# Fourteen mixed-input tiles transposed by VectorE and transfers instead of TensorE, and a last projection in two column halves

## The chip, the cores and the metric

The kernel runs on one core of a Trainium2 chip. The metric is the device time of one execution in microseconds (us), given as the median of several runs. Engines are named as in the profile: PE is TensorE's matmul, PEld its weight load, DVE is VectorE, ACT is ScalarE, POOL is GpSimd, SP is SyncE. "ACTq" and "SPq" are the sequencers of ACT and SP, on which their DMAs are issued.

## What is computed

The reference adds two terms to `x` (64 sequences of 32 tokens of 512 numbers). The first mixes the 32 tokens of a sequence by one of 16 condition matrices. The second is attention of the result over a paged cache of 512 keys plus the 32 new ones, with 32 query heads and 8 key heads of 128.

```python
x = x + einsum('bct,bcd->bdt', x, weights[condition])        # the mix: x1
q, k, v = x1 @ Wq.T, x1 @ Wk.T, x1 @ Wv.T                    # q, k: rmsnorm, then rope
k_all = concat([k_cache[block_table], k]); v_all likewise    # cache masked beyond its length
o = softmax(q @ k_all / sqrt(128)) @ v_all
x = x1 + o @ Wo.T
```

## The kernel before

All data are float32. The 64 sequences are taken four at a time, as tiles of 128 tokens: 16 tiles. Each tile is worked on twice, once for each half of the heads (`hh` is 0 or 1), so there are 32 steps; `st.n` counts them, and steps 0 to 15 are the first half. In a step the four sequences of the tile are four batches (`bt`), and each batch has four key heads (`g`), which makes 16 slots (`slot = bt * GH + g`). Every slot has the scores and the values of one batch and head. Into the slots the kernel places, by hand, the work of other steps: the projections of the step after this one (`ahead`, through `pieces`: rotation tables in slot 2, `k_a` in slot 3, the query projections `q_a` in slots 4 to 7, `v_a` in slot 13), the output projection of the step before in slots 8 and 9, and the mixed input of the step after next (`beyond`) in slots 14 and 15.

The order of instructions on PE and SP is the order in which the program writes them (`manual_schedule`); DVE, ACT and POOL are ordered by a scheduler. A DMA that SP issues is held until the data that it needs are there, and everything behind it on SP's queue waits too. The program gives DMAs of SP and ACT eight semaphores in turn; a DMA waits until the one that had its semaphore before has landed.

These parts matter here:

- `x1_a` loads a tile of `x` into `acc`. `x1_c` (slot 14) multiplies it on PE by a block-diagonal matrix `bd` of four conditions (L363) and DVE adds the product to `acc` (L364). `acc` now holds x1 with tokens on the partitions.
- `x1_b` (slot 15) makes `x1t`, x1 with its 512 columns on the partitions in four blocks of 128: four PE transposes (L371), an ACT copy out of PSUM (L373), and an ACT-issued DMA that keeps it in device memory for the second half of the heads (`x1t_d`, L374).
- `x1_t` (slot 13) loads `x1t` again for a step of the second half (L357). For a step of the first half it does nothing.
- `project` multiplies `x1t`, as the stationary operand, by a weight tile (L407). `k_a` in slot 3 of the next step is its first user.
- `load_k`, called when a `Batch` is made, has SP load 16 pages of 64 KB of cached keys (L294) into one of two buffers; page numbers come by a register load (L286). The keys are copied to DVE-written tiles by `head_keys` (L567) one batch ahead of their use. The batch made at `bt == 3` has half of its pages issued in slot 13.
- `turn_rows` (L457) and `spread` (L471) already turn the queries of steps 2 and later by DVE in 32x32 blocks, and SP transfers put the blocks in place.
- The tile tag `w1` is one buffer, used by `norm_rope`, the rotation angles and `count`.
- The last output projection runs after the loop, all 512 columns at once (L520). Three quarters through it calls `in_range`, which counts the softmax denominators that are in range, sums the counts on PE (L1020) and writes the flag `redo` (L1021). DVE then adds the projection to `acc` (L528) and SP stores it (L533). All engines read `redo` and branch on it; the slower exact version behind the branch is not run here.

Of the kernel before, what the change touches and what calls it, by code (L numbers as in the profile page):

```python
# [11 lines left out]
F32 = mybir.dt.float32  # L12
I32 = mybir.dt.int32
AF = mybir.ActivationFunctionType
ALU = mybir.AluOpType
# [4 lines left out]
P = 128  # L20
B, S, HID = 64, 32, 512
D, HQ, HK = 128, 32, 8
REP = HQ // HK
PAGES, PSIZE, NPP = 64, 32, 16
# [31 lines left out]
def cond_resid_paged_attention_kernel(  # L56
# [130 lines left out]
    def steps_of(exact, pools):  # L187
# [164 lines left out]

        def x1_t(st):

            if st.hh:
                st.x1t = work.tile([P, KC, P], F32, tag="x1t", name=f"x1t_{st.name}", bufs=1)
                nc.sync.dma_start(st.x1t.rearrange("p c q -> p (c q)"), x1t_d[st.t])  # L357

        def x1_c(st):
            if st.hh:  # L360
# [5 lines left out]
        def x1_b(st):  # L366
            if st.hh:
                return
            pm = ps_p.tile([P, KC, P], F32, tag="pp", name=f"px1t_{st.name}")
            for c in range(KC):  # L370
                nc.tensor.transpose(pm[:, c, :], st.acc[:, c * P : (c + 1) * P], ident)  # L371
            st.x1t = work.tile([P, KC, P], F32, tag="x1t", name=f"x1t_{st.name}", bufs=1)
            nc.scalar.copy(st.x1t, pm)  # L373
            nc.scalar.dma_start(x1t_d[st.t], st.x1t.rearrange("p c q -> p (c q)"))  # L374

        def rot_tables(st):

# [98 lines left out]
        def by_tensor(st):  # L476
            return st.n < 2 or exact
# [32 lines left out]
        def q_b(st, g):  # L510
            to_columns(st, g)

        def out_proj(st, part, halfway=None):

            if part.start == 0:
                st.po = ps_p.tile([P, HID], F32, tag="pp", name=f"pout_{st.name}")
            for i in range(part.start, part.stop):
                if halfway and i == 3 * QH // 4:
                    halfway()
                nc.tensor.matmul(  # L520
                    st.po,
                    st.ot[:, i, :],
                    wt["o", st.hh, i // 4][:, i % 4, :],
                    start=(i == 0),
                    stop=(i == QH - 1),
                )
            if part.stop == QH:
                nc.vector.tensor_tensor(st.acc, st.po, st.acc, ALU.add)  # L528
                if exact or st is steps[-1]:
                    store(st)  # L530

        def store(st):
            nc.sync.dma_start(  # L533
                out[st.t * P : (st.t + 1) * P, :] if st.hh else acc_d[st.t], st.acc
            )

        def new_ot(st):
            st.ot = act.tile([P, QH, P], F32, tag="ot", name=f"ot_{st.name}", bufs=1)
# [192 lines left out]
        if exact:  # L731
            nc.gpsimd.memset(vn_bufs[0], 0.0)
            nc.gpsimd.memset(vn_bufs[1], 0.0)
            key_no = wpool.tile([P, LK], F32, tag="key_no", name="key_no")
            key_no_i = work.tile([P, LK], I32, tag="sm", name="key_no_i")
            nc.gpsimd.iota(key_no_i, pattern=[[1, LK]], base=0, channel_multiplier=0)
            nc.vector.tensor_copy(key_no, key_no_i)
            nc.vector.memset(key_no[:, L:LK], -1e9)
            for st in steps:
                if st.t == 0:  # L740
                    load_w("k", st.hh)
                    load_w("v", st.hh)
                    for g in range(GH):
                        load_w("q", st.hh, g)
                        load_w("o", st.hh, g)
                if not st.hh:
                    load_cond_weights(st.t)
                x1_a(st)
                x1_t(st)
                x1_c(st)  # L750
                x1_b(st)
                rot_tables(st)
                k_a(st)
                k_b(st)
                v_a(st)
                for g in range(GH):
                    q_a(st, g)
                    q_b(st, g)
                new_ot(st)
                for bt in range(BT):  # L760
                    exact_batch(Batch(st, bt), key_no)
                out_proj(st, slice(0, QH))
            return
# [163 lines left out]
        for st in steps:  # L927
            ahead = steps[st.n + 1] if st.n + 1 < len(steps) else None
            beyond = steps[st.n + 2] if st.n + 2 < len(steps) else None
            fill = pieces(ahead) if ahead else {}  # L930
            for bt in range(0 if st.n else 1, BT):
                this, after = batch, None
                n = st.n * BT + bt + 2
                if n < NHH * NT * BT:
                    after = Batch(steps[n // BT], n % BT, NPP // 2 if bt == BT - 1 else NPP)
                    unfilled += [(after, c) for c in range(VC)]
                for g in range(GH):
                    slot = bt * GH + g
                    if st.n or slot > GH:
                        scores(this, g)  # L940
                    if slot == 0:
                        new_scores(st)
                    if slot in (1, 3):
                        new_values(st, slot - 1)
                    if slot < GH and valued is not None:
                        values(*valued)
                    for piece in fill.get(slot, ()):
                        if isinstance(piece, tuple):
                            piece[0](ahead, piece[1])
                        else:  # L950
                            piece(ahead)
                    if slot in (8, 9) and st.n:
                        out_proj(steps[st.n - 1], slice((slot - 8) * QH // 2, (slot - 7) * QH // 2))
                    if slot == 9:
                        if st.n:
                            new_ot(st)
                        for ba in turned:
                            turn(ba)
                        turned = []
                        if 0 < st.n < NT // TRIG - 1:  # L960
                            tmp = work.tile(
                                [P, 3, TRIG * HD], F32, tag="w1", name=f"trig_{st.n}", bufs=1
                            )
                            with tc.issue_after(last["dve"]), tc.issue_after(last["act"]):
                                angles((st.n + 1) * TRIG, tmp)
                    if slot == 10 and st.n:
                        store(steps[st.n - 1])
                    if st.n and beyond:
                        if slot == 6 and not beyond.hh:
                            load_cond_weights(beyond.t)  # L970
                        if slot == 11:
                            x1_a(beyond)
                    if slot == 13:
                        if beyond:
                            x1_t(beyond)
                        for load in after.pages_left if after else ():
                            load()
                    if slot == 14 and beyond:
                        x1_c(beyond)
                    if slot == 15 and beyond:  # L980
                        x1_b(beyond)
                    if slot == 1 and st.n == NT:
                        count(0)
                    if st.n == 1 and slot in (4, 5):
                        load_parts(outputs, 0, slot + 2)
                    for at in second_outputs.get((st.n - NT, slot), ()):
                        load_parts(outputs, 1, at)
                    if st.n in (NT - 2, NT - 1):
                        load_parts(
                            [("k", 0), ("q", 0), ("q", 1), ("q", 2), ("q", 3), ("v", 0)],  # L990
                            1,
                            slot - 5 + (st.n - NT + 2) * BT * GH,
                        )
                    for _ in range({1: 0, GH: 2}.get(slot, 1)):
                        if unfilled and (g or unfilled[0][0] is this):
                            next_values()
                    if slot >= GH and valued is not None:
                        values(*valued)
                    valued = this, g
                    if g == 1 and bt != 1:  # L1000
                        for ba in turned:
                            turn(ba)
                        turned = []
                    if later is not None:
                        head_keys(later, g)
                turned.append(this)
                batch, later = later, after
# [14 lines left out]
                redo, pc, float(P * NHH * NT * BT * GH), None, ALU.not_equal  # L1022
            )

        out_proj(steps[-1], slice(0, QH), in_range)

    redo = const.tile([1, 1], I32, tag="redo", name="redo")
    run(False)
# [54 lines left out]
```

## Time and profile before

| | |
|---|---|
| device time, median of 3 runs | 2170.74 us (2169.95 to 2174.28) |
| the profiled execution's own time | 2166.54 us |
| span of the profiled execution | 2164.8 us |
| PE busy | 2145.4 us, 99% |
| DVE, ACT, POOL busy | 1196.6, 863.0, 805.5 us |
| DMA engines, mean | 165 GB/s; 35.1% of their time for SP's queue, 22.3% for POOL's |
| granted TensorE clock | 0.997 |

The page lists the busy time of each engine, 40 slices of the span, the DMA queues, the chain of work that ended last, and groups of instructions. A group's row gives the line, the engine, the operation, the tile it writes and those it reads, the count, the busy time in us and the mean time of one in ns. PE's matmuls overlap in the records: one can last 0.27 us in its row while the next starts 0.11 us after it. What one costs is therefore read from the starts of its neighbours. A DMA's row gives the time that its issue took, not that of its data. When the data have landed is read from the times at which its semaphore was counted up in the trace.

### The profile page before, as it was taken

What the parts mean: (1) busy time and instruction counts of PE and PEld (TensorE: products, weight loads), DVE (VectorE), ACT (ScalarE), POOL (GpSimd) and SP (SyncE); (2) the same over time, 40 slices, a digit from 0 to 9 for tenths busy, and PEclk for the clock granted to TensorE, in tenths of its full rate; (3) what the DMA queues carried; (4) which work ended last, traced back from release to release, by engine and by line L of the source; (5) the groups of instructions that cost most, each with busy time, mean ns of one, the idle gap of its engine ahead of it and who ended that gap; (6) DMA issues with size and microseconds to landing.
All of it is one profiled execution on the core that took longest, in us unless ns stands there. A gap on an engine that the chain in (4) does not pass through costs nothing.

```text
span 2164.8 us, 41582 instructions
## 1 busy us (share of the span) xinstructions
PE 2145.4 (99%) x12990; PEld 1497.4 (69%) x12990; DVE 1196.6 (55%) x2884; ACT 863.0 (40%) x1576; POOL 805.5 (37%) x1009
## 2 busy tenths in 40 slices
PE   8999999999999999999999999999999999999998
PEld 5766777667776677766777766777667777667775
DVE  5666555665455564555654565644655545556442
ACT  3444444444433343333443333433334433334441
POOL 4433333433333343333433334333334333334330
PEclk9999999999999999999999999999999999999999
DMA  8665565555655556556766855565555555555651
GB/s 250 188 165 160 157 169 160 143 159 158 173 153 153 154 156 173 156 151 190 229 181 178 207 161 162 164 177 156 155 144 168 165 167 165 147 159 162 172 158 59
DMA packets 386839, 357.47 MB, mean 165 GB/s; under 512 B 54480, under 2 KB 316640, under 8 KB 386608
## 3 DMA queue, kind: packets, MB, share of 16 engines
q1 hardware_dynamic: 341616, 212.74, 35.1%
q0 software_dynamic: 41984, 137.71, 22.3%
q10 hardware_dynamic: 3008, 4.25, 0.5%
q8 instruction: 106, 1.74, 0.3%
q14 instruction: 125, 1.02, 0.2%
HBM read 302.59 MB, written 12.58 MB: 146 GB/s over the span
## 4 chain that ended last, share of the span: by engine, by line
PE 97%; DVE 1%; DMA 1%; ACT 0%; issue 0%; POOL 0%; DVEq 0%; ACTq 0%
PE po_x L632 22%; PE ps_x L574 21%; PE pout_x L520 20%; PE pp_q_x L407 20%; PE pp_v_x L407 5%; PE pp_k_x L407 5%; PE pnv_x L616 2%; PE psn_x L592 1%; PE pmix_x L363 1%; DMA pages_at<-in_pages_v_dram 1%; PE px1t_x L371 0%; DMA cond<-in_cond_dram 0%; PE pt_x L451 0%; ACT sq_q_x L417 0%; ACT q_cols_x L491 0%
## 5 line engine op out<-in xcount | busy, mean ns | idle before, releaser
L321 POOL DMA_INDIRECT raw_x<-in_vc_dram,v_row x512 | 539.6, 1054 | 821.5 <-ACT v_x L334 757.0
L582 ACT ACTIVATE pr_x<-ps_x 128x512 f32<-128x512 f32 x512 | 305.7, 597 | 822.7 <-PE ps_x L574 819.3
L632 PEld LDWEIGHTS po_x<-v_x,pr_x 128*128 128x128 f32 x4096 | 515.7, 192 | 123.9 <-issue 112.5
L632 PE MATMUL po_x<-v_x,pr_x 128*128 128x129 f32 x4096 | 550.6, 278 | 0.0
L407 PE MATMUL pp_q_x<-wq_x,x1t_x 128*128 128x512 f32 x1024 | 462.2, 594 | 0.0
L520 PE MATMUL pout_x<-wo_x,ot_x 128*128 128x512 f32 x1024 | 450.2, 593 | 0.0
L574 PE MATMUL ps_x<-q_cols_x,kh_x 128*128 128x128 f32 x3072 | 406.0, 275 | 1.6 <-ACT q_cols_x L491 1.6
L574 PEld LDWEIGHTS ps_x<-q_cols_x,kh_x 128*128 128x128 f32 x3072 | 376.3, 192 | 18.0 <-issue 14.5
L334 ACT ACTIVATE v_x<-raw_x,valid 128x512 f32<-128x512 f32 x512 | 363.2, 716 | 13.4 <-DMA raw_x<-in_vc_dram,v_row 13.2
L520 PEld LDWEIGHTS pout_x<-wo_x,ot_x 128*128 128x128 f32 x1024 | 190.0, 191 | 214.0 <-issue 213.8
L567 DVE COPY kh_x<-k_t_x 128x512 f32<-128x512 f32 x506 | 206.8, 418 | 194.6 <-PE ps_x L574 153.5
L407 PEld LDWEIGHTS pp_q_x<-wq_x,x1t_x 128*128 128x128 f32 x1024 | 185.8, 191 | 184.8 <-issue 184.8
L650 DVE TENSOR_TENSOR nv_x<-po_x,nv_x 128x258 f32<-128x258 f32 x256 | 108.6, 424 | 309.4 <-PE po_x L632 294.0
L424 POOL TENSOR_TENSOR rs_q_x<-ms_q_x,minus_half 128x4 f32<-128x4 f32 x128 | 140.0, 1094 | 168.9 <-DVE ms_q_x L422 168.9
L417 ACT ACTIVATE sq_q_x<-pp_q_x 128x512 f32<-128x512 f32 x128 | 76.4, 597 | 266.2 <-PE pp_q_x L407 179.3
L574 PE MATMUL ps_x<-q_last_x,kh_x 128*128 128x128 f32 x1024 | 135.3, 275 | 0.0
L528 DVE TENSOR_TENSOR acc_x<-pout_x,acc_x 128x512 f32<-128x512 f32 x32 | 22.2, 692 | 199.3 <-PE pout_x L520 199.3
L574 PEld LDWEIGHTS ps_x<-q_last_x,kh_x 128*128 128x128 f32 x1024 | 124.6, 192 | 0.0
L407 PE MATMUL pp_v_x<-wv_x,x1t_x 128*128 128x512 f32 x256 | 115.2, 593 | 0.0
L407 PE MATMUL pp_k_x<-wk_x,x1t_x 128*128 128x512 f32 x256 | 115.1, 593 | 0.0
L653 DVE TENSOR_TENSOR o_x<-nv_x,rden 128x256 f32<-128x256 f32 x256 | 108.8, 425 | 6.2
L421 DVE TENSOR_REDUCE ms_q_x<-sq_q_x 128x4 f32<-128x512 f32 x128 | 86.3, 674 | 45.4 <-ACT sq_q_x L417 44.8
(107 smaller groups left out, 1464.8 us busy)
## 6 DMA issues: line engine op xcount, KB each, us to landing
k_t_x<-in_kt_dram SPq DMA_DIRECT2D x2048, 64.0 KB
q_cols_x<-rows_x SPq DMA_DIRECT2D x360, 80.0 KB
q_last_x<-rows_x SPq DMA_DIRECT2D x120, 80.0 KB
raw_x<-in_vc_dram,v_row POOLq DMA_INDIRECT x512, 4.2
wo_x<-in_wo_dram SPq DMA_DIRECT2D x32, 256.0 KB
acc_x<-in_x_dram SPq DMA_DIRECT2D x16, 256.0 KB
x1t_d<-x1t_x ACTq DMA_DIRECT2D x16, 256.0 KB
acc_d<-acc_x SPq DMA_DIRECT2D x16, 256.0 KB
```

The costliest lines, as they stand in the source:

```text
L321: nc.gpsimd.indirect_dma_start(out=raw.rearrange("p g d -> p (g d)"), out_offset=None, in_=vc, in_offset=bass.IndirectOffsetOnAxis(ap=v_ro ...
L334: nc.scalar.activation(v_bufs[b % 2][:, c, :, 0:D], raw, AF.Copy, scale=ok)
L407: nc.tensor.matmul(pp, st.x1t[:, c, :], w[:, c, :], start=(c == 0), stop=(c == KC - 1))
L421: nc.vector.tensor_reduce(ms, sq, AX.X, ALU.add)
L424: nc.gpsimd.tensor_tensor(rs, ms, minus_half, ALU.pow)
L520: nc.tensor.matmul(st.po, st.ot[:, i, :], wt["o", st.hh, i // 4][:, i % 4, :], start=(i == 0), stop=(i == QH - 1),)
L567: last["dve"] = nc.vector.tensor_copy(k, ba.k_raw[:, :, g, :]).ins
L574: nc.tensor.matmul(ps[:, c, :], ba.k[g][:, c * P : (c + 1) * P], queries(ba, g), start=True, stop=True,)
L582: last["act"] = nc.scalar.activation(pr, ps, AF.Exp, scale=SCALE).ins
L632: nc.tensor.matmul(ba.po[:, g % 2, :], ba.pr[g][:, c, :], ba.v_t[:, c, g, :], start=(c == 0), stop=(c == VC - 1),)
L650: nc.vector.tensor_tensor(t, ba.po, t, ALU.add)
L653: nc.vector.tensor_tensor(ba.o[:, both, :], t[:, :, 0:D], rd.unsqueeze(2).to_broadcast([P, 2, D]), ALU.mult,)
```

## The change

For the first-half steps from number 2 on (14 of them), `x1_b` no longer uses PE and ACT. DVE transposes `acc` in 32x32 blocks into a tile of tag `w1`, and SP writes the blocks to `x1t_d` by four DMAs, one for each group of 32 partitions. Each puts 512 pieces of 32 numbers (128 bytes) in their places, so that `x1t_d` holds the full transpose. `x1_t` then loads `x1t` from there for these steps too. It stands at the start of the next step, between page 4 and page 5 of the keys that are loaded there (`bt == 0`); before, all 16 pages were issued in one go. Steps 0 and 1 keep the PE transposes, and the loads for the second half keep their place in slot 13.

The last output projection is done as two halves of 256 columns, each with its own DVE add and its own store. `in_range` is called three quarters through the first half.

```diff
         def x1_t(st):
-            if st.hh:
-                st.x1t = work.tile([P, KC, P], F32, tag="x1t", name=f"x1t_{st.name}", bufs=1)
-                nc.sync.dma_start(st.x1t.rearrange("p c q -> p (c q)"), x1t_d[st.t])
+            st.x1t = work.tile([P, KC, P], F32, tag="x1t", name=f"x1t_{st.name}", bufs=1)
+            nc.sync.dma_start(st.x1t.rearrange("p c q -> p (c q)"), x1t_d[st.t])
...
         def x1_b(st):
             if st.hh:
                 return
+            if not by_tensor(st):
+                return x1_turn(st)
...
+        def x1_turn(st):
+            turned = work.tile([P, KC * BT, S], F32, tag="w1", name=f"x1w_{st.name}", bufs=1)
+            nc.vector.transpose(turned, st.acc.rearrange("p (j d) -> p j d", d=S))
+            kept = x1t_d[st.t].rearrange("(j d) (c b x) -> b d c j x", d=S, b=BT, x=S)
+            for b in range(BT):
+                nc.sync.dma_start(
+                    kept[b],
+                    turned[b * S : (b + 1) * S, :, :].rearrange("p (c j) x -> p c j x", c=KC),
+                )
...
-        def out_proj(st, part, halfway=None):
+        def out_proj(st, part, cols=slice(0, HID), halfway=None):
...
                 nc.tensor.matmul(
-                    st.po,
+                    st.po[:, cols],
                     st.ot[:, i, :],
-                    wt["o", st.hh, i // 4][:, i % 4, :],
+                    wt["o", st.hh, i // 4][:, i % 4, cols],
...
-                nc.vector.tensor_tensor(st.acc, st.po, st.acc, ALU.add)
+                nc.vector.tensor_tensor(st.acc[:, cols], st.po[:, cols], st.acc[:, cols], ALU.add)
                 if exact or st is steps[-1]:
-                    store(st)
+                    store(st, cols)
...
             for bt in range(0 if st.n else 1, BT):
...
+                back = bt == 0 and ahead and not ahead.hh
                 if n < NHH * NT * BT:
-                    after = Batch(steps[n // BT], n % BT, NPP // 2 if bt == BT - 1 else NPP)
+                    after = Batch(
+                        steps[n // BT],
+                        n % BT,
+                        NPP // 4 if back else NPP // 2 if bt == BT - 1 else NPP,
+                    )
+                    if back:
+                        x1_t(ahead)
+                        for load in after.pages_left:
+                            load()
...
                     if slot == 13:
-                        if beyond:
+                        if beyond and beyond.hh:
                             x1_t(beyond)
...
-        out_proj(steps[-1], slice(0, QH), in_range)
+        out_proj(steps[-1], slice(0, QH), slice(0, HID // 2), in_range)
+        out_proj(steps[-1], slice(0, QH), slice(HID // 2, HID))
```

More of the change, by code (lines that the diff above doesn't have):

```diff
@@ L511, in q_b @@
             to_columns(st, g)
-        def out_proj(st, part, halfway=None):
-            if part.start == 0:
+        def out_proj(st, part, cols=slice(0, HID), halfway=None):
+            if part.start == 0 and cols.start == 0:
                 st.po = ps_p.tile([P, HID], F32, tag="pp", name=f"pout_{st.name}")
@@ L527, in out_proj, with store @@
             if part.stop == QH:
-                nc.vector.tensor_tensor(st.acc, st.po, st.acc, ALU.add)
+                nc.vector.tensor_tensor(st.acc[:, cols], st.po[:, cols], st.acc[:, cols], ALU.add)
                 if exact or st is steps[-1]:
-                    store(st)
[L532 to L535, printed above, removed]
+                    store(st, cols)
+        def store(st, cols=slice(0, HID)):
+            dst = out[st.t * P : (st.t + 1) * P, :] if st.hh else acc_d[st.t]
+            nc.sync.dma_start(dst[:, cols], st.acc[:, cols])
         def new_ot(st):
@@ L748, in steps_of @@
                 x1_a(st)
-                x1_t(st)
+                if st.hh:
+                    x1_t(st)
                 x1_c(st)
```

## The prediction

> **What bounds the kernel now.** I read the busy times first, then the chain of what ended last, then a window over the steps, and last the timeline of the slot that is changed.
>
> ```profile
> PE 2145.4 (99%) x12990; PEld 1497.4 (69%) x12990; DVE 1196.6 (55%) x2884; ACT 863.0 (40%) x1576; POOL 805.5 (37%) x1009
> ...
> PE 97%; DVE 1%; DMA 1%; ACT 0%; issue 0%; POOL 0%; DVEq 0%; ACTq 0%
> ```
>
> A busy share alone proves little, because matmul records overlap. The window over steps 2 to 14 (columns: window, length, busy time of PE, PEld, DVE, ACT, POOL with counts, clock, DMA share, GB/s) settles it: PE has no gap in 870 us.
>
> ```profile
> 170.00:1040.00 870.00, 870.00 (x5262) 605.47 (x5261) 491.12 (x1175) 357.14 (x648) 323.82 (x402) 1.00 0.57 162
> ```
>
> So work taken off PE is gained one to one, and anything that makes PE wait is lost one to one. Timeline of slots 14 to 16 and of the next step's `k_a` (start, length, engine, line):
>
> ```profile
> 502.74 0.69 DVE L364 TENSOR_TENSOR acc_x<-pmix_x,acc_x 128x512 f32<-128x512 f32 x1 [0.44 <-DMA k_t_x<-in_kt_dram]
> 503.43 1.06 PE L574 MATMUL ps_x<-q_last_x,kh_x 128*128 128x128 f32 x8
> 504.32 0.60 PE L371 MATMUL px1t_x<-ident,acc_x 128*128 128x128 f32 x4
> 504.75 1.06 PE L632 MATMUL po_x<-v_x,pr_x 128*128 128x129 f32 x8
> ...
> 515.71 1.88 PE L407 MATMUL pp_k_x<-wk_x,x1t_x 128*128 128x512 f32 x4
> ```
>
> The four transposes hold PE from 504.32 to 504.75: 0.43 us. x1 is complete at 503.43 and `x1t` is first needed by the weight load ahead of 515.71, at 515.60. These 12.17 us are what a route through device memory may take. They are 12.1 to 12.2 us in 13 of the 14 steps.
>
> [...] only loads of 128 bytes are here, of 11 ns a packet. [...] an `x1t` load lasts 0.37 us in its row and lands 3.3 us after its start.
>
> **PE's gain.** 14 steps lose four transposes: 14 x 0.43 = 6.0 us. ACT loses 14 copies (0.58) and DMA issues (0.33); it is busy 40% and nothing of PE waits for it, so that is worth nothing.
>
> **DVE.** It gains 14 transposes of 128x512, by the nearest row 0.70 us each. DVE runs at 55%; queued behind it are the adds, head copies and output turns of slot 15. The buffer freed by the add at L650 is used again about 6 us later and the key copies a batch later, so a shift of 0.7 us costs nothing. Without that cover it would be 9.8 us. The turned tile takes the one `w1` buffer; its next user in slot 4 comes some 17 us after x1 is complete, later than the four writes that read it.
>
> ```profile
> L663 DVE STREAM_TRANSPOSE ot_x<-o_x 128x512 f32<-128x512 f32 x127 | 86.1, 697 | 1.2
> ...
> L471 SPq DMA_DIRECT2D q_cols_x<-rows_x x360: 507/588/1577, 144.1 to 2085.8; - x180
> ...
> L357 SPq DMA_DIRECT2D x1t_x<-x1t_d x16: 331/372/402, 1040.2 to 2026.8; - x16
> ...
> L286 SPq TENSOR_LOAD <-pages_sb x128: 967/1004/1742, 7.1 to 2106.5; - x128
> ...
> 501.67 4.56 SPq L294 DMA_DIRECT2D k_t_x<-in_kt_dram  x8
> ```
>
> **SP's new chain**, from the moment x1 is complete (503.43 in the step shown):
> - SP is still issuing slot 13's pages until 506.23, so +2.8; over the steps from 4 on 2.6 to 4.4, mean 3.0. This hides the DVE transpose, done by +0.8.
> - Four writes. Nearest row: the spread, also from 32 partitions, 0.59 plus a gap of 0.04; from below a plain store, 0.38 with gap. I take the spread: 2.5, so +5.5.
> - The register load of the next batch, L286. Its median is 1.0, but at this boundary mostly 1.5 to 1.7; I take 1.5, and 0.26 to the first page: +7.3.
> - Four pages at a spacing of 0.51: +9.35. Here the load of `x1t` is issued, if the writes have landed.
> - Landing: the 16 loads of the second half took 2.6 to 4.9 us, median 3.3: +12.65.
>
> PE needs it at 12.17 - 0.43 = 11.74. It is **0.9 us late**, and PE waits, with nothing to do in its order behind it: 14 x 0.9 = 12.6 us. The ends: plain-store issue, register load of 1.0 and landing in 2.65 give 3.0 + 1.5 + 1.26 + 2.06 + 2.65 = +10.5, early by 1.2, cost 0. The upper ends of register load and landing give about +14.6, late by 2.9, cost 40.
>
> The writes: the fourth starts at +4.9 and holds nothing if it has landed by +9.35. Stores of the same 256 KB in one DMA (L374) took 2.0 to 5.5 us. The 14 x 2048 pieces are 128 for each of 16 DMA engines per step; at 11 ns they take 1.4 us and are hidden.
>
> The twelve remaining pages follow the load: issued by +15.9, where before the sixteenth was issued at +16.1 (519.5), because SP stood waiting for ACT's write:
>
> ```profile
> SPq L294 <- DMA x1t_d<-x1t_x: 33.2, 16, 6.5
> ```
>
> That wait goes (33 us of SP, none of it PE's), and the new one takes its place; the keys come no later. POOL's queue is not touched.
>
> **The end.** 32 half matmuls for 16: PE turns over a 128-column weight load and matmul in 0.11 us, so half the columns take half the time, and the projection stays 13.7 us. The last DVE add shrinks from 0.69 to about 0.42 (L650, 258 columns): 0.27. The count is 5.15 us sooner (12 of 32 pieces instead of 24). At the end POOL drains for 8.57 us after its branch, to 2163.91, and SP is done at 2162.56. If that drain only starts sooner, 1.35 more is gained; if it waits for something else, nothing. 0.3 to 1.6; I take 1.0.
>
> **Sum**, against the profiled execution of 2166.5: - 6.0 - 1.0 + 12.6 = + 5.6, 2172.1. The median of the runs lies 4.2 above that execution: 2170.7 + 5.6 = **2176.3 us**. 0.2% (4.3 us) is about what a measurement can tell from no change here.
>
> **Rivals.** *Hidden.* The load is there in time and only the gain is left: 2170.7 - 7.0 = 2163.7. For it: the page loads issued at that moment landed mostly in 1.8 to 2.5 us, near their fastest, and the chain's low end is 1.2 us early. Against it: the medians say late, and instruction fetches of 16 KB held SP's issue for 1 to 2 us in half of the steps near there. It decides if the chain comes to 11.74: for instance writes of 0.43 each with the gap, register load 1.25, pages 2.06 and 3.3 for landing, with little jitter. Chance 0.33.
>
> *Slow pieces.* 128-byte writes to device memory hold the load. They decide from (9.35 - 3.85) / 128 = 43 ns a piece and engine. At 64 ns they end at 12.0, the load lands near 15.5, 3.8 late, 53 us: about 2217. At the 86 ns of a 2048-byte packet: about 2257. Against it: 11 ns for loads. [...] Chance 0.2 with every other delay above 2 us a step.
>
> *Late keys.* Priced above at nothing; DVE already waits 25 us for pages without PE noticing. It needs pages over 5 us later. It lies in the 0.2.
>
> That the change doesn't do what it says is excluded: PE's order without the transposes and SP's with the four writes, the load and the twelve pages follow from the code.
>
> **Numbers.** Forecast 0.47: late by 0.3 to 2 us a step, 2168 to 2192. Hidden 0.33: 2161.5 to 2166.5. Slow 0.2: above 2192. Faster by over 0.2%: 0.28 of hidden and 0.01 = 0.29. Within: 0.05 + 0.11 + 0.04 = 0.20. Slower: 0.35 + 0.16 = 0.51. The range runs from 2162 to 2204, which leaves out the worst half of the slow case and the edge of the hidden one. Both signs are likely; the forecast's own range is 2168 to 2192.
>
> **What would show it.** In the profile after: a wait of PE's weight load at `k_a` for the DMA into `x1t`, 14 times of about 0.9 us (none: hidden; over 2: slow pieces); SP waiting ahead of that load for the writes (long: slow pieces); no px1t beyond steps 0 and 1; about 10 us more of DVE. The forecast is wrong if PE has no gap in the steps of the first half.

## The result and the profile after

The changed kernel takes 2182.59 us in the median of 7 runs (2178.88 to 2189.57), the kernel before 2171.41 us (7 runs, the three of the table above among them): ratio 1.0057, interval 1.0047 to 1.0066. It is slower by about 12 us. Its profiled execution took 2179.96 us, with a span of 2178.2 us. Lines have moved: in the changed kernel the mix's add is L363, the DVE turn L381, the four writes L384, the load of `x1t` L356, `k_a` (and the other projections) L420, the page loads L294 as before, the last projection L533 with its add L541.

The page of the kernel after: busy times, the chain of what ended last, and the group of `k_a`'s matmuls (busy us, mean ns | idle time before them, and what ended it).

```profile
PE 2144.7 (98%) x12966; PEld 1498.1 (69%) x12966; DVE 1205.7 (55%) x2899; ACT 860.1 (39%) x1562; POOL 804.8 (37%) x1009
...
PE 91%; SPq 3%; DMA 2%; issue 1%; DVE 1%; ACT 1%; POOL 0%; DVEq 0%; ACTq 0%
...
L420 PE MATMUL pp_k_x<-wk_x,x1t_x 128*128 128x512 f32 x256 | 118.8, 607 | 11.5 <-DMA x1t_x<-x1t_d 9.0
```

PE's share of the chain fell from 97% to 91%, and SP's queue and DMAs now have 5% together, where they had 1%. The row of `k_a` had no idle time before; now it has 11.5 us, most of it put down to the load of `x1t`. (The page counts from the modelled end of the matmul before; by the starts of the matmuls, which are used below, the same waits come to 13.5 us.) The rest of the 11.5 us is put down to ACT's copies `nv` and `v`, but those had long been done when PE went on: the load was what came last there too. The window over steps 2 to 14 of the kernel after says the same, with PE busy 858.63 of 870 us:

```profile
170.00:1040.00 870.00, 858.63 (x5141) 592.66 (x5140) 494.43 (x1179) 346.51 (x625) 319.13 (x398) 1.00 0.58 162
```

The timeline of the same step as in the prediction, from the mix to `k_a`:

```profile
506.23 3.43 SPq L294 DMA_DIRECT2D k_t_x<-in_kt_dram  x7
...
506.82 0.69 DVE L363 TENSOR_TENSOR acc_x<-pmix_x,acc_x 128x512 f32<-128x512 f32 x1 [0.44 <-PE pmix_x L362]
...
507.61 0.71 DVE L381 STREAM_TRANSPOSE x1w_x<-acc_x 128x512 f32<-128x512 f32 x1
...
509.76 3.50 SPq L384 DMA_DIRECT2D x1t_d<-x1w_x  x4
...
514.65 1.90 SPq L294 DMA_DIRECT2D k_t_x<-in_kt_dram  x4
...
516.74 0.33 SPq L356 DMA_DIRECT2D x1t_x<-x1t_d  x1
...
519.64 1.52 PE L420 MATMUL pp_k_x<-wk_x,x1t_x 128*128 128x512 f32 x3
```

x1 is complete at 507.51 and turned at 508.32, but SP issues pages until 509.66, then the four writes, a register load, four pages, and only at 516.74 the load, which lands at 519.51; PE goes on at 519.64. That is 0.3 us late, and this is one of the mild steps: over the 14 the wait is between nothing and 2.8 us. And SP's waits (us in total, times, longest):

```profile
SPq L294 <- DMA x1t_d<-x1t_x: 5.5, 1, 5.5
...
SPq L356 <- DMA x1t_d<-x1w_x: 2.4, 4, 1.0
```

The old wait for ACT's write has gone from 33.2 to 5.5 us. The new one, ahead of the load, is 2.4 us in all, in 4 waits: in at least ten of the 14 steps the writes had landed.

When the starts of PE's groups are laid beside those of the kernel before, one profiled execution against the other, the 13.4 us between them fall into these parts:

| part | us | forecast |
|---|---|---|
| transposes gone, 14 x 0.44 | - 6.1 | - 6.0 |
| PE waiting at the 14 `k_a` | + 13.5 | + 12.6 |
| slower matmuls just after those waits | + 2.7 | none |
| last projection and end | - 1.2 | - 1.0 |
| first 105 us (startup) | + 1.5 | none |
| second half of the heads, up to the last projection | + 3.0 | none |

The last two rows are not of the change: the experiments below show them in kernels that don't have it, or with another size in each execution. The 1.5 us of the start arise between 60.37 and 63.79 us, where the granted clock is 0.50 in this trace and 1.00 in the profile of before.

In the third row 1.8 us come from one place. After a wait of 2.84 us PE ran its next four matmuls at 0.85 us apiece instead of 0.43. Two windows there (the third figure from the end of a row is the granted clock):

```profile
995.50:999.00 3.50, 3.48 (x5) 1.42 (x6) 0.00 (x0) 0.00 (x0) 0.00 (x0) 0.52 0.72 216
999.50:1003.00 3.50, 3.50 (x16) 2.07 (x15) 1.45 (x4) 1.73 (x4) 0.08 (x1) 1.00 0.29 82
```

The clock was 0.52 for 3.5 us, though PE was busy in them, and 1.00 again afterwards. The mean over the execution, 0.997 as before, doesn't show it. The other 0.9 us are 0.07 us between the first two matmuls of each of the other 13 `k_a`.

The end of the kernel after:

```profile
2161.09 1.99 PE L533 MATMUL pout_x<-wo_x,ot_x 128*128 128x256 f32 x8
...
2163.12 0.42 DVE L541 TENSOR_TENSOR acc_x<-pout_x,acc_x 128x256 f32<-128x256 f32 x1 [1.78 <-PE pout_x L533]
...
2163.60 7.17 PE L533 MATMUL pout_x<-wo_x,ot_x 128*128 128x256 f32 x32 [0.52 <-DVE acc_x L541]
2170.81 0.42 DVE L541 TENSOR_TENSOR acc_x<-pout_x,acc_x 128x256 f32<-128x256 f32 x1 [7.27 <-PE pout_x L533]
```

Both halves lie in one PSUM tile, so the second half of the matmuls stood still until DVE had read the first: the last of the first half ends its turn at 2162.92, the next starts at 2163.60. From its first to its last matmul the projection took 1.1 us longer, 0.7 us of it by this wait. Against that, the stretch from the last matmul's start to the end of the span is 7.8 us instead of 10.1. POOL's drain again took 8.57 us, but it began 5.8 us before the last matmul, where it had begun 0.7 us after it, and so it no longer ends last: the last store landed 3.6 us after the last matmul's start, and SP's closing waits took another 4.2 us.

### The profile page after: what moved, and what is told of

Read it like the earlier page. It is cut to its first block, busy times and chain, and to the rows that moved or that the text cites. A ratio compares the mean times of both kernels' runs of the same rounds, so it can differ in the third digit from the quotient of the medians.

```text
span 2178.2 us, 41737 instructions
## 1 busy us (share of the span) xinstructions
PE 2144.7 (98%) x12966; PEld 1498.1 (69%) x12966; DVE 1205.7 (55%) x2899; ACT 860.1 (39%) x1562; POOL 804.8 (37%) x1009
## 4 chain that ended last, share of the span: by engine, by line
PE 91%; SPq 3%; DMA 2%; issue 1%; DVE 1%; ACT 1%; POOL 0%; DVEq 0%; ACTq 0%
PE pout_x L533 20%; PE pp_q_x L420 20%; PE po_x L644 19%; PE ps_x L586 19%; PE pp_k_x L420 5%; PE pp_v_x L420 4%; PE pnv_x L628 2%; SPq L294 2%; PE psn_x L604 1%; DMA x1t_x<-x1t_d 1%; SPq L384 1%; SPq L484 1%; DMA pages_at<-in_pages_v_dram 1%; DMA x1t_d<-x1w_x 0%; SPq L286 0%
## 5 line engine op out<-in xcount | busy, mean ns | idle before, releaser
L420 PE MATMUL pp_q_x<-wq_x,x1t_x 128*128 128x512 f32 x1024 | 461.3, 593 | 0.0
L533 PE MATMUL pout_x<-wo_x,ot_x 128*128 128x512 f32 (+1 forms) x1056 | 450.5, 580 | 0.5 <-DVE acc_x L541 0.5
L533 PEld LDWEIGHTS pout_x<-wo_x,ot_x 128*128 128x128 f32 x1056 | 195.7, 190 | 210.0 <-issue 207.6
L420 PEld LDWEIGHTS pp_q_x<-wq_x,x1t_x 128*128 128x128 f32 x1024 | 185.2, 191 | 184.5 <-issue 184.0
L541 DVE TENSOR_TENSOR acc_x<-pout_x,acc_x 128x512 f32<-128x512 f32 (+1 forms) x33 | 22.3, 676 | 204.8 <-PE pout_x L533 204.8
L420 PE MATMUL pp_k_x<-wk_x,x1t_x 128*128 128x512 f32 x256 | 118.8, 607 | 11.5 <-DMA x1t_x<-x1t_d 9.0
L420 PE MATMUL pp_v_x<-wv_x,x1t_x 128*128 128x512 f32 x256 | 115.2, 592 | 0.0
L434 DVE TENSOR_REDUCE ms_k_x<-sq_k_x 128x4 f32<-128x512 f32 x32 | 22.0, 686 | 163.2 <-ACT sq_k_x L430 163.2
```

Source lines behind the costliest of these rows:

```text
L420: nc.tensor.matmul(pp, st.x1t[:, c, :], w[:, c, :], start=(c == 0), stop=(c == KC - 1))
L434: nc.vector.tensor_reduce(ms, sq, AX.X, ALU.add)
L533: nc.tensor.matmul(st.po[:, cols], st.ot[:, i, :], wt["o", st.hh, i // 4][:, i % 4, cols], start=(i == 0), stop=(i == QH - 1),)
```

## The experiments

The theory after the comparison: the new route costs what SP's queue makes it cost. The load stands behind pages, writes, a register load and pages again, and lands a microsecond too late; neither the small pieces nor DVE matter. The rivals: the route is slow by itself (small writes, landing times), the second part of the change carries a share, or the profile of before was an unusual execution. The last projection alone, the route alone, the load behind eight pages and the writes between the groups of pages ran on one chip (kernel before: 2170.21 us, 28 runs), the other four on another (2166.76 us, 24 runs), so ratios are compared.

**The last projection alone.** The kernel before with `out_proj` and its two calls from the change.

```diff
-        out_proj(steps[-1], slice(0, QH), in_range)
+        out_proj(steps[-1], slice(0, QH), slice(0, HID // 2), in_range)
+        out_proj(steps[-1], slice(0, QH), slice(HID // 2, HID))
```

> The kernel before, with only the last projection in two halves of columns (the count sooner); mixed input as before. From the trace of the change: the projection takes 1.1 us longer on PE (0.68 of it a wait of the second half for DVE's add of the first), the stretch from the last matmul to the end is 2.3 us shorter, because POOL's drain of 8.57 us starts sooner. Theory: 1.2 us less than the kernel before, ratio 0.9995 (no difference that can be measured). The prediction had 1.0 us less, with the whole of it at the end and none lost on PE. Rival: the end is set by the landing of the last store and nothing is won; then 1.1 us more, 1.0005. The profile tells them apart: last matmul 1.1 us later, tail near 7.8 us instead of 10.1.

Measured: 2170.35 us, ratio 0.9999 (0.9991 to 1.0008): no difference that can be measured. In its profile the projection is 1.1 us longer, as in the change, and the stretch from the last matmul to the end is 8.7 us, 1.4 less than before; in other kernels with the halves it is 6.5 to 8.3. The gain at the end is real but varies. It is not the landing of the last store that varies (3.5 to 3.9 us after the last matmul's start in all of them), but SP's closing waits behind it, 2.8 to 4.9 us; why, is open. About half of the gain is paid for on PE by this wait, 0.7 us by the starts:

```profile
PE pout_x L520 <- DVE acc_x L528: 0.5, 1, 0.5
```

This kernel has no new route, yet its trace too has 3.0 us more than the profile of before in the second half of the heads and 1.6 us more at the start.

**The route alone.** The change with the last projection of the kernel before (the diff above, turned round).

> The change with the last projection of the kernel before: only the 14 mixed inputs go by VectorE and device memory. Theory: it carries the whole loss, 2182.6 + 1.2 = 2183.8 us, ratio 1.0062. In its profile PE is late at the 14 first key projections by 13 to 15 us in sum, less 6.1 us for the transposes. Rival for the rest of the loss (the trace of the change has 1.5 us more before 70 us, 0.9 us more in the second half and one stall of 2.0 us at 2110 us, in which neither part of the change lies): if these are noise of one execution, they are at other places or absent here, and the ratio is nearer 1.004; if they belong to the new program, they come at the same places again.

Measured: 2182.99 us, ratio 1.0074 (1.0055 to 1.0092). The route carries the whole loss. Here PE waits 17.0 us in sum at the 14 `k_a`, less 6.1 us; once more one wait, this time of 2.50 us, is followed by half-rate matmuls (1.8 us), while waits of 2.41 and 2.82 us are not (the traces at two of these waits stand below, with the half rate). The 3.0 us of the second half are here again, most of them in one stall at the same slot of the last step, and the start has none: the second half's share is the same with and without the route, the start's varies.

**The load behind eight pages.**

```diff
-                        NPP // 4 if back else NPP // 2 if bt == BT - 1 else NPP,
+                        NPP // 2 if back else NPP // 2 if bt == BT - 1 else NPP,
```

> The change with the load of the turned tile behind eight pages of the next keys on SP's queue instead of four. Theory (place on SP's queue decides): the load is issued 4 x 0.51 = 2.06 us later, so each of 14 waits grows from 1.0 to about 3.1 us: 29 us more, 2211 us. Second part of the theory: in the change's profile, the one wait of 2.8 us was followed by four matmuls at half the rate, 1.8 us more; if every wait of about 3 us brings that, 14 x 1.8 = 25 us come on top: 2236 us, ratio 1.030. Rival (the landing of the small writes decides, or the transfers in flight): four pages more in front change little, below 2190 us.

Measured: 2239.33 us, ratio 1.0318 (1.0303 to 1.0333). Both parts of the theory show. The group of `k_a` on its page:

```profile
L420 PE MATMUL pp_k_x<-wk_x,x1t_x 128*128 128x512 f32 x256 | 143.4, 713 | 52.2 <-DMA x1t_x<-x1t_d 52.2
```

The load is issued 12.12 us after x1 is complete instead of 9.80, and takes 3.6 us to PE's start instead of 3.0, so the waits come to 54 us instead of 13.5: 41 us more, where 29 were expected. All 14 waits are of 2.81 us or more, and each is followed by matmuls at half rate: the mean of a matmul rises from 607 to 713 ns, and the steps lose 27 us that way (25 expected). Four page issues of 0.5 us, moved, cost 57 us.

**The load ahead of all pages.** `0 if back` in the same line.

> The change with the load of the turned tile ahead of all pages of the next keys. Theory: SP now stands still until the fourth write has landed (it starts at +4.9 and took 4.2 us in the median: +9.1), so only about 0.4 us are gained of the 2.06 us of four pages; lateness 0.3 to 0.6 us instead of 1.0: about 7 us less than the change, 2175 us, ratio 1.002. SP's wait for the writes grows from 2.4 us in sum to 14 x 1 to 2 us. Rival (the writes would long have landed and only the four pages stood in the way): 2.06 us sooner, all waits gone, 2167 us, ratio 0.998.

Measured: 2170.96 us, ratio 1.0017 (1.0008 to 1.0026), the ratio of the theory, and not the rival. By the starts PE waits 9.7 us in sum, 0.7 us a step where 0.3 to 0.6 were expected; one wait of 2.83 us is again followed by matmuls at half rate. Waits of PE at the load, and of SP at the writes:

```profile
PE pp_k_x L420 <- DMA x1t_x<-x1t_d: 6.4, 6, 2.7
```

```profile
SPq L356 <- DMA x1t_d<-x1w_x: 25.4, 25, 2.5
```

With no page in front, the load is issued at 9.4 us after x1 instead of 9.8: now SP stands still until the writes have landed. Their landing (4.2 us median from the start of a write) is hidden behind the four pages of the change only just: in the change the load was issued 0.1 to 1.2 us after the fourth write had landed.

**The writes on ACT's queue.**

```diff
-                nc.sync.dma_start(
+                nc.scalar.dma_start(
                     kept[b],
```

> The change with the four writes issued by ACT instead of SP; the load stays behind four pages on SP. Theory (place on SP's queue decides): SP's chain loses 4 x 0.63 = 2.5 us, the load is issued near +6.8 to +8 instead of +9.4 and lands before +11: the 14 waits go, 2182.6 - 15.3 = 2167 us, ratio 0.998. Rival (ACT has no room at that place): four issues of 0.6 us stand ahead of the exponentials that the value products wait for; PE then waits for pr up to 1.5 us a step, 21 us, and the sum is near 2188 us, ratio 1.008.

Measured: 2200.24 us, ratio 1.0155 (1.0141 to 1.0169): the rival, and worse than it. PE's waits, then SP's, then ACT's timeline:

```profile
PE pnv_x L628 <- ACT pn_x L612: 20.6, 14, 3.0
PE pp_k_x L420 <- DMA x1t_x<-x1t_d: 11.2, 11, 1.8
```

```profile
SPq L294 <- DMA x1t_d<-x1w_x: 43.0, 14, 3.7
```

```profile
521.81 4.42 ACTq L384 DMA_DIRECT2D x1t_d<-x1w_x  x3
526.27 0.72 ACT L334 ACTIVATE v_x<-raw_x,valid 128x512 f32<-128x512 f32 x1 [3.89 <-DMA x1t_d<-x1w_x]
```

ACT stands at the writes for over 4 us, and the exponentials behind them come late for PE, in each of the 14 steps. It is not the four issues alone that hold it: in the step shown the fourth write takes the semaphore of the second, and is issued at 525.65, when that one has landed (525.63). The 20.6 us are the rival's 21; what it did not count is that the waits at `k_a` stay (13.0 us by the starts), and that three of the waits for the exponentials, 3.0, 2.4 and 1.9 us long, are followed by a stretch at half rate. And SP gained nothing: writes and pages take the same eight semaphores in turn, so SP's pages now wait for the writes to land, 43 us in all, and the load is issued at 10.0 us after x1 as ever. Through the semaphores the writes still stood in SP's way.

**The writes between the two groups of pages.** Mix and turn move to slot 13, behind the value projection; SP issues the writes after the first eight pages of the batch, and the load behind the second eight. Slots 14 and 15 keep steps 0 and 1.

```diff
-                    if back:
-                        x1_t(ahead)
-                        for load in after.pages_left:
-                            load()
...
                     if slot == 13:
                         if beyond and beyond.hh:
                             x1_t(beyond)
+                        turned_here = beyond and not by_tensor(beyond) and not beyond.hh
+                        if turned_here:
+                            x1_c(beyond)
+                            x1_b(beyond)
                         for load in after.pages_left if after else ():
                             load()
+                        if turned_here:
+                            x1_t(beyond)
```

> The change with the mix and the turn one to two slots sooner (slot 13, after the value projection), so that SP issues the four writes between the two groups of eight pages and the load right behind the second group, ahead of the next register load. Theory (SP's queue is what made it late): the load is issued near 4 us sooner against the need, all 14 waits go, 13.5 + 1.8 us: 2182.6 - 15.3 = 2167 us, ratio 0.998. Rival 1 (writes of 128-byte pieces and a load from device memory are too slow by themselves): waits stay, above 2176. Rival 2 (eight pages 2.6 us later starve the keys, or PE waits for the mixed tile's load): new waits of PE elsewhere, above 2172.

Measured: 2165.88 us, ratio 0.9978 (0.997 to 0.9986), where 0.998 was expected. Of the 14 waits at `k_a` two are left (0.7 and 0.8 us by the starts, against 13.5 in all before); the same number of DMAs of the same size goes the same way. Two things have changed at once, though: x1 is complete 13.7 us ahead of `k_a` (without its waits) instead of 11.8, because the mix stands in an earlier slot, and the load follows x1 after 8.8 us instead of 9.8, because of its place on the queue. Together the load is issued 2.9 us sooner against the need, where near 4 were expected, and no run tells whether one of the two alone would have been enough. That the place on the queue counts by itself is shown by the load behind eight pages. Rival 2 has a small share, since the tile of x now comes late at times:

```profile
PE pmix_x L362 <- DMA acc_x<-in_x_dram: 1.5, 3, 1.1
...
PE pp_k_x L420 <- DMA x1t_x<-x1t_d: 0.5, 1, 0.5
```

**The same, with two more edits.** The tile of x is loaded in slot 10 behind the store, and the second half of the last projection gets a PSUM tile of its own.

```diff
-            if part.start == 0 and cols.start == 0:
+            if part.start == 0:
                 st.po = ps_p.tile([P, HID], F32, tag="pp", name=f"pout_{st.name}")
...
                     if slot == 10 and st.n:
                         store(steps[st.n - 1])
+                        if beyond and not beyond.hh:
+                            x1_a(beyond)
...
-                        if slot == 11:
+                        if slot == 11 and beyond.hh:
                             x1_a(beyond)
```

> The version with the writes between the two groups of pages, with two more edits: the tile of x is loaded one slot sooner (right behind the store of slot 10), and the second half of the last projection has its own PSUM tile. In the trace of the version without these edits PE still waits for the mixed tile's load and about it 2.8 us, for the load of x1t 1.5 us, and at the last projection 0.7 us for DVE's add. Theory: 3 to 4 us less than that version's 2165.9, so about 2162.5 us, ratio 0.9965. Rival (SP then waits for the store to land ahead of the spread of the queries, which comes later): new waits of PE for the queries, no gain, 2166 us.

Measured: 2159.19 us, ratio 0.9965 (0.9952 to 0.9979), the ratio expected, and faster than both kernels. SP and PE on its timeline, and its window over the steps:

```profile
499.97 0.69 DVE L363 TENSOR_TENSOR acc_x<-pmix_x,acc_x 128x512 f32<-128x512 f32 x1 [3.14 <-PE pmix_x L362]
...
501.50 2.66 SPq L384 DMA_DIRECT2D x1t_d<-x1w_x  x4
504.35 5.58 SPq L294 DMA_DIRECT2D k_t_x<-in_kt_dram  x8
510.03 0.39 SPq L356 DMA_DIRECT2D x1t_x<-x1t_d  x1
...
514.29 3.60 PE L420 MATMUL pp_k_x<-wk_x,x1t_x 128*128 128x512 f32 x8
```

```profile
170.00:1040.00 870.00, 870.00 (x5281) 604.98 (x5280) 502.13 (x1192) 355.17 (x641) 324.83 (x406) 1.00 0.60 168
```

The load is issued 4.3 us ahead of its use in this step, the eight pages hide the landing of the writes, and PE has no gap. SP does wait for the store to land, as the rival had it (21.1 us in 13 waits), but PE doesn't notice. Which of the two edits brought how much no run tells; the projection takes 0.8 us less with its own PSUM tile.

**The kernel before once more.**

> The kernel before once more, for a second profile of it. The profiled execution of before (2166.5 us) is faster than every other run of that kernel; the traces of the changed kernels show some 0.1 us more in most steps of the second half and a stall near 2 us about slot 5 of the last step. If those belong to most executions of any kernel, they show in this profile too, at the same places, and its time is near 2170 us; if they belong to the change, this profile has none of them.

Measured: 2167.59 us, ratio 1.0003 (0.9994 to 1.0011); profiled 2169.26 us. Its second half is the same as in the first profile of before (0.03 us), and so it is in the three changed kernels on this chip (0.3 us at most). The four on the other chip had 1.5 to 3.0 us there, whatever their edit, and the kernel before took 3.4 us more on that chip than on this one. So these 3 us are not of the change, and seem to go with the chip. What they are is open, and there is no profile of the kernel before that is known to come from that chip. The start is 2.9 us longer than in the first profile: it differs from one execution to the next.

## Why the prediction was right, and where it was off

The forecast was 2176.3 us with PE late at `k_a`; the range held the result, and the mechanism and its place were right.

- **PE's gain**: 6.1 us for 6.0.
- **ACT and DVE at nothing**: right. DVE is busy 9 us longer (turn 0.71 us each), and between 105 and 1050 us PE waits at `k_a` alone, not for keys or copies.
- **SP's chain**, in us after x1 is complete, means over the 14 steps:

| | forecast | measured |
|---|---|---|
| last page issued | 3.0 | 2.5 |
| four writes issued | 5.5 | 5.8 |
| first page of the next batch | 7.3 | 7.3 |
| load issued | 9.35 | 9.8 |
| `k_a` starts (no wait: 11.7) | 12.65 | 12.8 |

The end of this chain fits better than its parts, by luck: the load was issued 0.45 us later than forecast and reached PE in 3.0 us where 3.3 had been put.

- **The writes**: taken as landed before the load's turn, and they were, with 2.4 us of SP waiting in 14 steps; the forecast had no number for how near it was. The fourth starts at 5.1 and lands 4.1 us later in the mean, at 9.2, against 9.8. *Slow pieces* are excluded: the 28672 packets of 128 bytes took 13 ns in the median in the trace, far from the 43 ns from which they would have decided.
- **The twelve pages and the keys**: no cost, as said. SP's wait for ACT's write went.
- **The end**: 1.2 us for 1.0, but the step "the projection stays 13.7 us" failed. It took 14.7, mostly because the second half waits for DVE's add in the shared PSUM tile, and the gain at the end was larger, 2.3 us. That the two come near 1.0 together is luck: in the trace of the halves alone they leave 0.3 us.
- **The sum**: + 5.6 forecast, about + 12 measured. The term that was mis-sized is the cost of being late, 14 x 0.9 = 12.6. The waits themselves came to 13.5 us in one execution and 17.0 in another, because a mean of 0.9 hides steps with none and steps of 2.8. And the waits cost more than their length: 2.7 us in the profile after, which the sum didn't have. With - 6.1, - 1.2, 13.5 to 17.0 and 2.7 one gets + 8.9 to + 12.4, where the medians differ by 11.2 us and the ratio of 1.0057 makes 12.4. The 13.4 us between the two profiled executions agree with that only by chance, since 4.5 us of them are startup and second half.
- **Rivals**: *hidden* failed in this kernel, but by a microsecond a step, and the version that moves the writes makes it true. The point from which it decides, a chain of 11.74 us, was well placed.

On the half rate: in the profiles of before and after, the granted clock fell to 0.50 three times in all between 20 us and the last projection, each time for 3.41 us (from 28.58 us before, from 60.37 and 995.63 us after), and was 1.00 again behind that. From 105 us to the last projection, in the ten traces together, 20 waits of PE of 1.9 us or more were followed by half rate: one of 2.84 us in the kernel after, one of 2.50 with the route alone, one of 2.83 with the load ahead of all pages, three of 1.9 to 3.0 with the writes on ACT's queue, and the 14 of 2.81 or more with the load behind eight pages. The length of a wait did not decide alone: with the route alone, waits of 2.41 and 2.82 us were not followed by it. In that kernel, at the wait of 2.50 us, PE's records fill 1.07 of 3.41 us, and in the next 3.41 us the clock is 0.50 (first two rows); at the wait of 2.82 us they fill 2.41 and 1.76 of two such stretches, and the clock stays at 1.00 in both (third and fourth row):

```profile
315.11:318.52 3.41, 1.07 (x4) 0.49 (x3) 0.00 (x0) 1.13 (x3) 0.94 (x1) 1.00 0.79 243
318.52:321.93 3.41, 3.41 (x5) 1.35 (x4) 0.00 (x0) 0.00 (x0) 0.00 (x0) 0.50 0.69 205
926.09:929.50 3.41, 2.41 (x30) 1.98 (x29) 1.23 (x4) 2.41 (x7) 0.98 (x1) 1.00 0.52 137
929.50:932.91 3.41, 1.76 (x4) 0.87 (x5) 0.00 (x0) 0.19 (x1) 0.94 (x1) 1.00 0.84 260
```

What decides between the two is not shown. Ahead of 105 us half rate came behind less idle time too: in the profile after, PE's records fill 2.46 of the 3.41 us from 56.96 us on, and the clock is 0.50 from 60.37 us. What brought it on there is open. The prediction had late steps of 2 to 3 us in its own range, and no term for half rate.

## What to carry to other kernels

What this route through device memory took was set less by its transfers than by what stood ahead of them on the queue that issued them: four page issues of 0.5 us, moved ahead of the load, cost 57 us over 14 steps. Count every instruction there, and put independent transfers between a write and the load that needs it: SP waited 25.4 us for the writes with no page between, and 2.4 us with four. Let the producer of the operand stand earlier where it can: of the 2.9 us that the writes between the groups of pages won, 1.9 came from that. Where PE was the bound, the cost of a late operand was not linear here: 20 waits of 1.9 us and more were followed by half rate, and behind `k_a` this added 1.5 to 3.0 us to the wait. Before two profiles are subtracted, look whether a stage that the change doesn't touch differs too.

## What the runs showed of the hardware that was not expected

- Waits of PE were followed by half rate: behind 105 us, up to the last projection, 17 of the 18 waits of 2.8 us or more, and three of 1.9, 2.4 and 2.50 us, but not one of 2.41 us. In the kernel after, the clock was 0.50 for 3.41 us behind the wait of 2.84 us. The mean granted clock doesn't show it: it fell only from 0.997 to 0.986 with 14 such waits.
- DMAs of 128-byte pieces into device memory took 0.64 us to issue (512 pieces each) and 13 ns a packet. They landed 4.2 us after their start in the change (median). Issued between the two groups of pages, most of the first three of a step landed in 2.2 us, but the fourth, for which the load must wait too, took 3.4 to 5.8 us there as well.
- Moving the writes to ACT's queue did not free SP's, since both took their semaphores from one set: SP waited 3.1 us a step (43.0 us in 14 waits) for the writes of ACT.
